# A two-layer graph network on one core: another order for the attention quads of a turn, and norms taken graph by graph at the two ends

## The chip, the core and the metric

The kernel runs on one core of a Trainium2 chip. A core has separate engines with their own instruction streams: TensorE (matrix products, "PE" in the profile, with its weight loads as "PEld"), VectorE ("DVE"), ScalarE ("ACT"), GpSimd ("POOL"), and SyncE ("SP"), which here only issues transfers (DMAs). Engines wait for each other through semaphores. Products land in PSUM, where the kernel uses eight tiles of 128 x 512 floats; everything else lives in SBUF, with 128 partitions. All arithmetic is 32-bit.

The metric is the device time of one execution, in microseconds (us), as the median of several runs.

## The reference

Sixty-four graphs of 256 nodes with 256 features each, and an integer adjacency matrix per graph, go through two layers.

```python
# layer 0: two graph attentions, then a feed-forward block
def gat(h, adj, W, a):
    Wh = h @ W
    e = leaky_relu(Wh @ a[:F] + swapaxes(Wh @ a[F:], 1, 2), 0.2)
    att = softmax(where(adj > 0, e, -9e15), axis=1)
    return att @ Wh
h = layernorm(x + gat(gat(x, adj, W1, a1), adj, W2, a2))    # first norm
x = layernorm(h + relu(h @ w_ff1 + b_ff1) @ w_ff2 + b_ff2)  # second norm

# layer 1: attention with relations, 8 heads of 32
q, k = x @ Wq + bq, x @ Wk + bk
attn = softmax(q k^T / sqrt(32))
out = sum over r of (attn * (adj == r)) @ (x @ Wv[r] + bv[r])   # adj is 0 or 1: two relations count
x = layernorm(x + out @ Wo + bo)                            # third norm
x = layernorm(x + gelu(x @ W1 + b1) @ W2 + b2)              # fourth norm
```

The hidden width of both feed-forward blocks is 1024.

## The kernel before

The graphs are taken in 32 pairs, so that a tile of features holds 512 nodes. The program is a pipeline written by hand: a fill brings the first pairs up to their stages, then 32 turns follow. In one turn (`turn(y_, x_, z)`) three pairs are at work: pair Y does attention and feed-forward of layer 1, pair X, one later, the feed-forward block of layer 0, pair Z, two later, both graph attentions of layer 0. Turn 30 has no Z, turn 31 has neither X nor Z. In turns with X the order of the instructions on TensorE, SyncE, VectorE and ScalarE is the order of the calls in the code (`tc.manual_schedule`); in turn 31 and in the fill only TensorE's and SyncE's are, and a planner places the rest. GpSimd's is the planner's throughout.

The attention of layer 1 is worked off in four *quads*: quad n is one of the two graphs (n // 2) and four of the eight heads. Each quad has these steps:

- `scores(n)`: 16 products over 32 rows into four PSUM banks (`sp`, L1015), and four exponentials on ScalarE (`e`, L1021)
- `masks(n)`: two products with the adjacency on VectorE (`ea`, L1026)
- `totals(n)`: one addition over the two halves of the nodes on VectorE (`es`, L1031)
- `sums(n)`: 32 products of the exponentials with the values into `po` (L1041) and 8 products of the totals with ones into `zo` (L1044)
- `shares(b)`, once per graph: the division (`divided`, L1052 to L1058): two transposes, a reciprocal and a product on VectorE, and one small addition on GpSimd

`values` makes the value blocks `v`, one per 128 nodes (products L999, addition of the bias on VectorE L1001). `e` and `ea` have two buffers each.

The hidden layer of a feed-forward block (`hidden_seven`) uses seven half-size products in place of eight (Strassen's scheme), each in two halves a and b. Its steps are named by product and half: `2a` makes half a of product 2, and so on; `2`, `5` and `3` of a half share a PSUM bank (`h1b`), `1`, `6`, `7` and `4` another (`h1a`). After `2`, `5` and `3` ScalarE copies the bank out (`copied`, L880), after `1`, `6` and `7` VectorE adds (`added`, L883); a product that goes on in the bank waits for that. `r`, `s` and the end of `4` are the activations on ScalarE (L914, L889). Four subtractions on VectorE (`tt`, L854) stand ahead of `hidden_seven`. In the first layer the input `hT` is the transposed, normalised pair: VectorE transposes 32 x 32 blocks (`yt`, L668), four blocks are placed by GpSimd copies (L685), twelve by DMAs on SyncE's queue (L687).

`HiddenOut` is the output product of the block, seven products again (`yf`, L960, additions to `y` L968), with sums of quarters of the hidden layer as operands (`sums`, L946).

A norm is made of statistics on VectorE (`moments`, L801 and L802), the inverse deviation on GpSimd (`rs`, L812 and L813), the shift on VectorE (`nm`, L821) and one application per 128 nodes on ScalarE (`applied_norm`, L828). Multiplication with the scale (`times`, L837) and addition of the offset (`plus`, L840) stand apart. `to_features` transposes a normalised pair on TensorE (L653), block by block, and copies it out (L654).

Six PSUM banks are handed out in turn (`bank`) to all products but `po` and `zo`, which have one each.

In the changed part of a turn pair X's scaled `y` gets its offset by a DMA that accumulates (L1209), issued by GpSimd. `early(z)` transposes pair Z's features on VectorE (`xT`, L1069), and `project` multiplies them (`xpp`, L715), half a pair at a time. `piece` takes one part of the output product that an earlier turn left over; there are such parts only in turn 31.

Of the kernel before, what the change touches and what calls it, by code (L numbers as in the profile page):

```python
# [12 lines left out]
ALU = mybir.AluOpType  # L13
# [3 lines left out]
P = 128  # L17
# [368 lines left out]
def narrow_path(  # L386
# [21 lines left out]
    G = 2  # L408
# [638 lines left out]
    def divided(u, b, po, zo, oT):  # L1047


        rz = work.tile([P, KB * N], F32, tag="s" if u < NG - 1 else "yt", name=f"rz{u}_{b}", bufs=1)  # L1050
        rq = work.tile([P, KB * N // 32], F32, tag="rq", name=f"rq{u}_{b}")
        nc.vector.transpose(rz, zo)  # L1052
        nc.vector.reciprocal(rq, rz.rearrange("p (n r) -> p n r", r=32)[:, :, 0])  # L1053
        nc.gpsimd.tensor_add(low, low, rq)  # L1054
        yield
        nc.vector.transpose(rz.rearrange("p (n r) -> p n r", r=32),
                            rq[:, :, None].to_broadcast([P, KB * N // 32, 32]))
        mark[f"divided{b}"] = nc.vector.tensor_tensor(  # L1058
            oT[:, :, b * N:(b + 1) * N], po.rearrange("p (m n) -> p m n", m=KB),
            rz.rearrange("p (m n) -> p m n", m=KB), ALU.mult)  # L1060
# [39 lines left out]

    def second_sums(z):
        d = g[z]
        for b in range(G):
            add_blocks(z, "ygp", d["y"], b,
                       lambda t, k: d["m"].s[:, t // NB * NB + k, t % NB * P:(t % NB + 1) * P],
                       lambda b, k: d["hp"][:, b * NB + k, :F], NB)
            if b == 0:
                mv = moments(z, 0, d["y"], range(NB))
        return mv
# [45 lines left out]
    def turn(y_, x_, z):  # L1155
# [24 lines left out]
        def shares(b):  # L1180
            return divided(y_, b, *acc[b], oT)

# [15 lines left out]
        with order:  # L1198
# [7 lines left out]
            if X:  # L1206
                X["hT"] = normed_features(x_, 0, X["y"])
                times(X["y"], rg1)
                nc.gpsimd.dma_start(X["y"], rb1[:, None, :].to_broadcast([P, T, F]), accum_op=ALU.add)  # L1209
            scores(0)  # L1210
            if z + 1 < NG:
                load_x(z + 1)
            if waiting:
                applied_norm(waiting[0][1], *last)
            if X:
# [3 lines left out]
            if not X:  # L1219
                masks(0)  # L1220
                totals(0)
            if X:
                v = values(y_, hT, range(T // 2, T - 1), v)
            steps = first_hidden(x_) if X else None
            scores(1)
            if not X:
                v = values(y_, hT, range(T // 2, T), v)
            masks(1)
            if not X:
                totals(1)  # L1230
            sums(0)
            if X:
                scores(2)
                first("2a 1a")
                totals(1)
                first("2b")
                masks(2, (0,))
                first("5a")
                v = values(y_, hT, range(T - 1, T), v)
                first("3a 6a")  # L1240
                masks(2, (2,))
                sums(1)
                scores(3)
                first("5b")
                totals(2)
                if Z:
                    early(z)
                first("7a 1b")
                divide = shares(0)
                next(divide)  # L1250
                first("ra 3b 6b")
                next(divide, None)
                first("4a 7b")
                if Z:
                    project(z, range(0, T // 2))
                first("rb")
                first("sa sb")
            else:
                piece()
                scores(2)  # L1260
                sums(1)
                piece()
                with behind("out"):
                    for _ in shares(0):
                        pass
                masks(2)
                totals(2)
                scores(3)
                piece()
                piece()  # L1270
            masks(3)
            totals(3)
            first("4b")
            sums(2)
            sums(3)
            if X:
                out = HiddenOut(x_, 0, X["y"], X["h1"], wf2s, out_sums(x_, 0))
                out.sums(1)
                if Z:
                    out.sums(2)  # L1280
            for _ in shares(1):
                pass
            out_(0)
            mv = moments(y_, 2, y, range(NB))
            piece()
            if Z:
                project(z, range(T // 2, T))
            if Z:
                early_adjacency(z)
            elif X:  # L1290
                out(1, 2)
                out.sums(2)
            out_(1)
            piece()
            if Z:
                first_scores(z)
            n = norm(y_, 2, y, mv=mv)
            if Z:
# [111 lines left out]
    with tc.manual_schedule(engines={mybir.EngineType.PE, mybir.EngineType.SP}):  # L1410
# [11 lines left out]
        second_softmax(1)  # L1422
        applied_norm(g[0]["y"], *norm(0, 0, g[0]["y"], mv=second_sums(0)))
        next(fold)
# [10 lines left out]
        first.sums(1, 2, 4, 3)  # L1435
        first(1, 2, 5, 6, 3, 7, 4)
        normed(0, 1, g[0]["y"])
        g[1]["n"] = norm(1, 0, g[1]["y"], mv=second_sums(1))
# [59 lines left out]
```

## Time and profile before

| | |
|---|---|
| median of 7 runs | 3083.49 us (3081.68 to 3086.09) |
| profiled execution | 3084.93 us, span 3083.3 us |
| granted TensorE clock, mean | 0.993 |
| TensorE | 3037.4 us busy, 99% of the span |
| VectorE | 2561.0 us, 83% |
| ScalarE | 1602.2 us, 52% |
| GpSimd | 685.8 us, 22% |
| a turn, from query projection to query projection | 93.55 us in most turns |

The span runs from the first to the last instruction of the profiled execution. A busy engine isn't an engine at its peak: products are pipelined, and a product that streams a little late leaves no idle time in the profile, only a larger distance to the next start. In the timeline a line is a group of equal instructions: start, time from the first's start to the last's end, engine, line, operation, output and inputs, shape, number, and in brackets the idle time of the engine before it and what ended it. In the view of waits the columns are who waited for whom, total, number and longest.

The page's row of the clock that was granted to TensorE shows full speed nearly throughout, and transfers take a small share:

```
PEclk8999999999999999999999999999999999999999
DMA  5112121221122221212211212211222212122000
```

### The profile page before, as it was taken

The numbers are of one execution on the slowest core, as the hardware profiler recorded it, in microseconds if no ns is written. First come the engines' busy times: TensorE is split into PE (matmuls) and PEld (weight loads), VectorE is DVE, ScalarE is ACT, GpSimd is POOL, SyncE is SP. The second block draws the span as 40 slices with busy tenths as digits, with TensorE's granted clock in tenths as the row PEclk, the third lists the DMA queues.
The fourth block names the chain that finished last, engine by engine and source line by source line (L and its number), as shares of the span: only waits on it lengthen the run. The fifth ranks groups of instructions, "written<-read, shape, count | busy, mean of one in ns | idle before, by whom it ended". The sixth has DMA issues, their size and how long they took to land.

```text
span 3083.3 us, 56471 instructions
## 1 busy us (share of the span) xinstructions
PE 3037.4 (99%) x21432; PEld 2341.4 (76%) x21432; DVE 2561.0 (83%) x4855; ACT 1602.2 (52%) x3212; POOL 685.8 (22%) x919
## 2 busy tenths in 40 slices
PE   7999999999999999999999999999999999999998
PEld 6678877778777778777787777787777787777866
DVE  4688888888888888888888888888888888888876
ACT  4455545554545555555555455545455555555543
POOL 3122121222211221212222212222112212122200
PEclk8999999999999999999999999999999999999999
DMA  5112121221122221212211212211222212122000
GB/s 149 20 37 43 39 45 32 51 44 38 41 42 39 45 48 33 45 33 50 44 40 42 46 32 51 44 38 41 42 39 44 48 33 45 32 51 44 19 19 16
DMA packets 444358, 129.64 MB, mean 42 GB/s; under 512 B 365065, under 2 KB 443441, under 8 KB 444081
## 3 DMA queue, kind: packets, MB, share of 16 engines
q1 hardware_dynamic: 417664, 102.46, 15.8%
q0 software_dynamic: 17424, 17.30, 3.5%
q10 hardware_dynamic: 8992, 6.19, 0.8%
q8 instruction: 172, 2.82, 0.4%
q14 instruction: 106, 0.86, 0.1%
HBM read 57.04 MB, written 16.78 MB: 24 GB/s over the span
## 4 chain that ended last, share of the span: by engine, by line
PE 88%; DVE 8%; ACT 1%; DMA 1%; issue 1%; SPq 1%; POOL 0%; DVEq 0%; ACTq 0%; POOLq 0%
PE yf L960 22%; PE h1a L871 15%; PE h1b L871 11%; PE po L1041 7%; PE vp L999 7%; PE sp L1015 4%; PE yop L786 4%; PE xpp L715 4%; PE qp L986 3%; PE kp L986 3%; PE ygp L786 3%; PE hpp L775 2%; PE zo L1044 2%; DVE s L750 2%; DVE eaq L946 1%; DVE yt L668 1%
## 5 line engine op out<-in xcount | busy, mean ns | idle before, releaser
L1021 ACT ACTIVATE e<-sp 128x512 f32<-128x512 f32 x512 | 264.4, 602 | 263.1 <-PE sp L1015 210.9
L883 DVE TENSOR_TENSOR h<-h1a,h 128x512 f32<-128x512 f32 x384 | 264.6, 690 | 159.2 <-PE h1a L871 155.8
L880 ACT COPY h<-h1b 128x512 f32<-128x512 f32 x384 | 226.4, 590 | 247.2 <-PE h1b L871 240.3
L1026 DVE TENSOR_TENSOR ea<-e,aT 128x1024 f32<-128x1024 f32 x256 | 311.2, 1246 | 32.7 <-ACT e L1021 32.7
L828 ACT ACTIVATE y<-y,nm,rs 128x256 f32<-128x256 f32 x450 | 238.7, 597 | 119.3 <-DVE nm L821 115.0
L1054 POOL TENSOR_TENSOR low<-low,rq 128x16 f32<-128x16 f32 x64 | 13.7, 214 | 1063.0 <-DVE rq L1053 1063.0
L685 POOL COPY hT<-yt 32x256 f32<-32x256 f32 x244 | 208.1, 853 | 60.1 <-DVE yt L668 50.2
L999 PE MATMUL vp<-wv,hT 128*128 128x512 f32 x480 | 218.9, 599 | 0.0
L801 DVE BATCH_NORM_STATS2 st<-y 128x6 f32<-128x256 f32 x512 | 207.9, 408 | 5.6
L968 DVE TENSOR_TENSOR y<-yf,y 128x256 f32<-128x256 f32 x448 | 183.3, 409 | 34.6 <-PE yf L960 31.0
L812 POOL TENSOR_SCALAR rs<-mv 128x4 f32<-128x4 f32 (+1 forms) x130 | 31.4, 242 | 723.5 <-DVE mv L802 636.2
L914 ACT ACTIVATE h<-h,cols 128x512 f32<-128x512 f32 x256 | 168.5, 723 | 1.5 <-DVE h L883 1.1
L988 ACT ACTIVATE q<-qp,cols 128x512 f32<-128x512 f32 x64 | 44.0, 688 | 239.7 <-PE qp L986 239.7
L837 DVE TENSOR_TENSOR y<-y,rg 128x1024 f32<-128x1024 f32 (+1 forms) x130 | 162.0, 1246 | 2.2 <-ACT y L828 1.1
L999 PEld LDWEIGHTS vp<-wv,hT 128*128 128x128 f32 x480 | 88.7, 190 | 97.6 <-issue 88.9
L1015 PEld LDWEIGHTS sp<-q,k 32*128 32x128 f32 x2048 | 98.8, 184 | 77.7 <-issue 49.8
L1031 DVE TENSOR_TENSOR es<-e 128x1024 f32<-128x1024 f32 x128 | 155.7, 1216 | 0.0
L1015 PE MATMUL sp<-q,k 32*128 32x256 f32 x2048 | 153.5, 400 | 0.0
L677 POOL COPY hT<-yt 32x256 f32<-32x256 f32 x120 | 115.9, 966 | 168.1 <-DVE yt L668 164.3
L717 ACT COPY xp<-xpp 128x260 f32<-128x260 f32 x128 | 48.1, 376 | 196.5 <-PE xpp L715 196.5
L854 DVE TENSOR_TENSOR tt<-hT 128x256 f32<-128x256 f32 x122 | 51.5, 422 | 107.6 <-DMA hT<-yt 103.5
L1041 PE MATMUL po<-e,v 128*32 128x256 f32 x2048 | 136.3, 384 | 0.0
(250 smaller groups left out, 7403.5 us busy)
## 6 DMA issues: line engine op xcount, KB each, us to landing
hT<-yt SPq DMA_DIRECT2D x912, 32.0 KB, 2.0
y<-in_x_dram SPq DMA_DIRECT2D x32, 512.0 KB, 4.6
y<-rb POOLq DMA_DIRECT2D x31, 512.0 KB, 5.3
xq<-in_x_dram SPq DMA_DIRECT2D x240, 64.0 KB, 2.2
aq<-in_adj_dram SPq DMA_DIRECT2D x240, 64.0 KB, 2.4
out_dram<-y SPq DMA_DIRECT2D x30, 512.0 KB, 2.9
hT<-yt ACTq DMA_DIRECT2D x180, 32.0 KB, 1.9
wf<-in_L_gnn_w_ff_dram SPq DMA_DIRECT2D x2, 1024.0 KB, 7.2
```

The source lines that it names most:

```text
L685: nc.gpsimd.tensor_copy(to, at)
L786: nc.tensor.matmul(ps[:, i * F:(i + 1) * F], lhs(t, k), rhs(b, k), start=(k == 0), stop=(k == n - 1))
L828: mark["normed"] = nc.scalar.activation(y[:, t, :], y[:, t, :], AF.Identity, bias=nm[:, t:t + 1], scale=rs[:, t:t + 1])
L871: nc.tensor.matmul(ps[:, i * N:(i + 1) * N], w_[:, f * P:(f + 1) * P], m, start=first and i == 0, stop=True, skip_group_check=True)
L880: mark["copied"] = nc.scalar.copy(out(h, o, b), pair(ps))
L883: mark["added"] = nc.vector.tensor_tensor(out(h, o, b), pair(one[h]), out(h, o, b), ALU.add)
L960: nc.tensor.matmul(s.ps[n][:, i * F2:(i + 1) * F2], a[:, k, i * P:(i + 1) * P], w_[:, k, :], start=n in (1, 2, 5) and i == 0 and k == 0, s ...
L999: nc.tensor.matmul(ps, hT[k][:, t * P:(t + 1) * P], wvf[:, k, :], start=(k == 0), stop=(k == KB - 1))
L1015: nc.tensor.matmul(ps[a][:, j * N:(j + 1) * N], k_[hp, m, j0:j0 + P], q[hp, m, b * N:(b + 1) * N], start=True, stop=True)
L1021: mark[f"exp{b * KB + m}"] = nc.scalar.activation(e[:, a, :], ps[a], AF.Exp, scale=isd)
L1026: nc.vector.tensor_tensor(ea[:, a:a + 2, :], e[:, a:a + 2, :], ab[:, None, :].to_broadcast([P, 2, NB * N]), ALU.mult)
L1041: nc.tensor.matmul(po[hp, m * N:(m + 1) * N], vs[:, hp], w[:, a, j * N:(j + 1) * N], start=(n == 0), stop=(n == len(terms) - 1))
```

## The change

In turns with X the first part of the turn has another order. Before, `scores(2)` stood directly behind `sums(0)`, `scores(3)` behind `sums(1)`. After, `scores(2)` comes behind the steps 2a, 1a and 5a, and `scores(3)` behind 4a, 7b and rb. The fourth values block comes directly behind the third, the second quad's totals directly behind its masks, the transpose of Z's features ahead of those masks, the first graph's division in one piece behind `sums(1)`, and Z's first projection behind `totals(3)`. The offset of X's `y` is added by VectorE ahead of `scores(3)`, in place of the accumulating DMA. The waiting pair's norm is applied after the first quad's totals.

Turns with and without X now share one sequence of calls. In turns 30 and 31 the third norm is taken graph by graph: statistics, deviation and application of the first graph, then of the second. In the fill the first norm of pair 0 is taken graph by graph too, each graph directly behind its last sums, and the second norm's first graph before the last two output products.

```diff
@@ -1052,7 +1052,6 @@
         nc.vector.transpose(rz, zo)
         nc.vector.reciprocal(rq, rz.rearrange("p (n r) -> p n r", r=32)[:, :, 0])
         nc.gpsimd.tensor_add(low, low, rq)
-        yield
         nc.vector.transpose(rz.rearrange("p (n r) -> p n r", r=32),
                             rq[:, :, None].to_broadcast([P, KB * N // 32, 32]))
         mark[f"divided{b}"] = nc.vector.tensor_tensor(
@@ -1098,13 +1097,14 @@
         d = g[z]
         d["hp"] = gat_first(z, d["m"].s, d["xp"], None if blocks[0] == 0 else d["hp"], blocks)
 
-    def second_sums(z):
+    def second_sums(z, graphs=range(G)):
         d = g[z]
-        for b in range(G):
+        mv = None
+        for b in graphs:
             add_blocks(z, "ygp", d["y"], b,
                        lambda t, k: d["m"].s[:, t // NB * NB + k, t % NB * P:(t % NB + 1) * P],
                        lambda b, k: d["hp"][:, b * NB + k, :F], NB)
-            if b == 0:
+            if b == 0 and len(graphs) == G:
                 mv = moments(z, 0, d["y"], range(NB))
         return mv
 
@@ -1178,7 +1178,7 @@
             applied(b, m, v, *e.pop(n), *acc[b])
 
         def shares(b):
-            return divided(y_, b, *acc[b], oT)
+            divided(y_, b, *acc[b], oT)
 
         def out_(b):
             add_blocks(y_, "yop", y, b, lambda t, k: oT[:, k, t * P:(t + 1) * P],
@@ -1206,12 +1206,9 @@
             if X:
                 X["hT"] = normed_features(x_, 0, X["y"])
                 times(X["y"], rg1)
-                nc.gpsimd.dma_start(X["y"], rb1[:, None, :].to_broadcast([P, T, F]), accum_op=ALU.add)
             scores(0)
             if z + 1 < NG:
                 load_x(z + 1)
-            if waiting:
-                applied_norm(waiting[0][1], *last)
             if X:
                 masks(0)
                 totals(0)
@@ -1219,82 +1216,76 @@
             if not X:
                 masks(0)
                 totals(0)
+            if waiting:
+                applied_norm(waiting[0][1], *last)
             if X:
-                v = values(y_, hT, range(T // 2, T - 1), v)
+                v = values(y_, hT, range(T // 2, T), v)
             steps = first_hidden(x_) if X else None
             scores(1)
             if not X:
                 v = values(y_, hT, range(T // 2, T), v)
+            if Z:
+                early(z)
             masks(1)
+            totals(1)
+            sums(0)
+            first("2a 1a 5a", 1)
+            scores(2)
+            sums(1)
+            if X:
+                shares(0)
+            first("3a 6a", 1)
             if not X:
-                totals(1)
-            sums(0)
+                with behind("out"):
+                    shares(0)
+            masks(2, (0,))
+            first("2b 1b")
+            masks(2, (2,))
+            first("5b 7a 3b ra 6b")
+            totals(2)
+            first("4a 7b rb")
             if X:
-                scores(2)
-                first("2a 1a")
-                totals(1)
-                first("2b")
-                masks(2, (0,))
-                first("5a")
-                v = values(y_, hT, range(T - 1, T), v)
-                first("3a 6a")
-                masks(2, (2,))
-                sums(1)
-                scores(3)
-                first("5b")
-                totals(2)
-                if Z:
-                    early(z)
-                first("7a 1b")
-                divide = shares(0)
-                next(divide)
-                first("ra 3b 6b")
-                next(divide, None)
-                first("4a 7b")
-                if Z:
-                    project(z, range(0, T // 2))
-                first("rb")
-                first("sa sb")
-            else:
-                piece()
-                scores(2)
-                sums(1)
-                piece()
-                with behind("out"):
-                    for _ in shares(0):
-                        pass
-                masks(2)
-                totals(2)
-                scores(3)
-                piece()
-                piece()
+                plus(X["y"], rb1)
+            scores(3)
+            first("sa sb", 2)
             masks(3)
             totals(3)
+            if Z:
+                project(z, range(0, T // 2))
             first("4b")
             sums(2)
             sums(3)
+            if not Z:
+                shares(1)
             if X:
                 out = HiddenOut(x_, 0, X["y"], X["h1"], wf2s, out_sums(x_, 0))
-                out.sums(1)
                 if Z:
-                    out.sums(2)
-            for _ in shares(1):
-                pass
+                    out.sums(1, 2)
+            if Z:
+                shares(1)
             out_(0)
-            mv = moments(y_, 2, y, range(NB))
+            if Z:
+                mv = moments(y_, 2, y, range(NB))
+            else:
+                n = norm(y_, 2, y, range(NB))
             piece()
             if Z:
                 project(z, range(T // 2, T))
             if Z:
                 early_adjacency(z)
             elif X:
+                out.sums(1)
                 out(1, 2)
                 out.sums(2)
             out_(1)
             piece()
             if Z:
                 first_scores(z)
-            n = norm(y_, 2, y, mv=mv)
+            if Z:
+                n = norm(y_, 2, y, mv=mv)
+            else:
+                applied_norm(y, *n)
+                n = norm(y_, 2, y, range(NB, T))
             if Z:
                 out(1)
                 Z["m"].scores(0)
@@ -1420,7 +1411,9 @@
         first_sums(1)
         next(fold)
         second_softmax(1)
-        applied_norm(g[0]["y"], *norm(0, 0, g[0]["y"], mv=second_sums(0)))
+        for b in range(G):
+            second_sums(0, (b,))
+            normed(0, 0, g[0]["y"], range(b * NB, (b + 1) * NB))
         next(fold)
         g[0]["hT"] = to_features(g[0]["y"], "h1T0")
         with behind("summed"):
@@ -1433,8 +1426,10 @@
         first_hidden(0)("2a 1a 2b 1b 5a 5b 3a 3b 6a ra 6b rb 7a sa 7b sb 4a 4b")
         first = HiddenOut(0, 0, g[0]["y"], g[0]["h1"], wf2s, out_sums(0, 0))
         first.sums(1, 2, 4, 3)
-        first(1, 2, 5, 6, 3, 7, 4)
-        normed(0, 1, g[0]["y"])
+        first(1, 2, 5, 6, 3)
+        normed(0, 1, g[0]["y"], range(NB))
+        first(7, 4)
+        normed(0, 1, g[0]["y"], range(NB, T))
         g[1]["n"] = norm(1, 0, g[1]["y"], mv=second_sums(1))
         g[0]["hT"] = to_features(g[0]["y"], "h2T0")
         affine(g[0]["y"], rg2, rb2)
```

## The prediction

> **What bounds the kernel now.** I read the page first, then the view of TensorE's own waits, the chain of waits in order of time, and last the timeline of one whole turn on each engine.
>
> ```profile
> PE 3037.4 (99%) x21432; PEld 2341.4 (76%) x21432; DVE 2561.0 (83%) x4855; ACT 1602.2 (52%) x3212; POOL 685.8 (22%) x919
> PE 88%; DVE 8%; ACT 1%; DMA 1%; issue 1%; SPq 1%; POOL 0%; DVEq 0%; ACTq 0%; POOLq 0%
> ```
>
> TensorE bounds it: 99% busy, 88% of the chain. The change adds and removes no matmul, so it can only move short stretches in which TensorE gets nothing or streams late. TensorE's own waits, in total, times and longest:
>
> ```profile
> PE yf L960 <- DVE y L968: 4.1, 4, 1.5
> PE h1T0p L653 <- ACT y L828: 3.5, 1, 3.5
> PE h1b L871 <- ACT e L1021: 3.4, 4, 0.9
> PE h2T0p L653 <- ACT y L828: 0.9, 4, 0.4
> PE h3T31p L653 <- ACT y L828: 0.8, 4, 0.3
> ```
>
> These are the waits the change touches; together some 13 us, or 0.4% of the run. Most of the loop's loss is smaller than an idle record, and shows as the distance between two starts. TensorE in turn 16:
>
> ```profile
> 1625.51 0.61 PE L1044 MATMUL zo<-es,ones 128*32 128x256 f32 x8
> 1626.05 1.15 PE L1015 MATMUL sp<-q,k 32*128 32x256 f32 x16
> 1627.15 1.11 PE L871 MATMUL h1b<-hT,wf 128*128 128x256 f32 x4
> 1628.10 1.03 PE L871 MATMUL h1a<-hT,wf 128*128 128x256 f32 x4
> 1628.96 1.03 PE L871 MATMUL h1b<-hT,wf 128*128 128x256 f32 x4
> 1629.86 1.13 PE L871 MATMUL h1b<-tt,wf1s 128*128 128x256 f32 x4
> 1630.83 1.88 PE L999 MATMUL vp<-wv,hT 128*128 128x512 f32 x4
> ...
> 1642.34 2.15 PE L871 MATMUL h1a<-tt,wf 128*128 128x256 f32 x8
> 1644.33 1.92 PE L715 MATMUL xpp<-gwe,xT 128*128 128x260 f32 x8
> ```
>
> Subtract neighbouring starts. An undisturbed step of four records takes 0.86 (1628.10 to 1628.96). Whatever is longer was late or changed the array's form. The same turn on the other engines:
>
> ```profile
> 1616.01 8.59 SPq L687 DMA_DIRECT2D hT<-yt  x12
> 1618.65 1.35 POOL L1209 DMA_DIRECT2D y<-rb  x1
> 1627.03 0.42 DVE L854 TENSOR_TENSOR tt<-hT 128x256 f32<-128x256 f32 x1 [3.19 <-DMA hT<-yt]
> 1604.09 1.22 DVE L840 TENSOR_TENSOR y<-y,rb 128x1024 f32<-128x1024 f32 x1
> ```
>
> The placing DMAs are issued until 1624.60, an accumulating 512 KB transfer goes out in the middle of them, and VectorE stands still for 3.19 until they land. Times "into the turn" below count from the first matmul of the query projection, here 1609.08.
>
> **The change, part by part.**
>
> *Bubbles that go.* (1) In the same view the second quad's scores, at 1622.46, take 1.30 to the next start, the third quad's 1.10: the fourth bank waits for VectorE's add of a values block; 0.2. (2) 5a starts 0.90 after 2b, the values block 0.97 after 5a, against 0.86: the copy of 2a stands on ScalarE behind the third quad's exponentials; 0.14. (3) The same at 3b behind the fourth quad's: the starts 1639.57, 1640.47, 1641.43 give 1.86 for two steps of 1.73; 0.14. (4) 6b to 4a 0.91; 0.05. (5) 4a and 7b take 1.99 for 1.73; 0.26. Sum 0.8 per turn.
>
> *Bubbles that come.* In the new order 5a, 5b and 3b each follow their bank's previous user after one step only. The second layer has that arrangement with an idle ScalarE: two steps h1b<-hT,w1s at 1678.62, next start 1680.42, 1.80 for 1.73. That is 0.08 for each, 0.24. 7b still stands one step behind an add: 0.22. Sum 0.46, so 0.33 is won.
>
> *Form changes.* Scores use 32 rows, sums 32 columns, all else the whole array. The half-length totals take 0.43 before more sums (1648.79 to 1649.22) and 0.54 before scores (1625.51 to 1626.05), also 0.55 before the output projection. The first step after scores takes 0.95 instead of 0.86, and scores 1.10 for passes worth 0.86. Before, second and third scores lay between sums and steps; after, scores lie between steps and sums, and sums between scores and steps. By these differences the three groups cost 1.2 now and 1.4 then: one whole form change more, 0.20 per turn. Net with the bubbles: -0.13 per turn, 31 turns: **-4.0**. Bounds: +0.2 if no bubble goes, -0.33 if the extra change is free: +6 to -10 in all. I take the middle, since each term has its own row.
>
> The Trainium skill, "TensorEngine Tiling (Array Packing)", section "Key Properties", speaks against the change: a change of tiling mode drains the array. It gives no price. At one equal price, 0.38 of a record less its 0.22 of pass, the added change would cost 0.16 per turn and the sum would be 1 us better than mine; the rows show unequal prices.
>
> *The accumulate becomes a VectorE add.* One 128x1024 add of 1.22, 31 times, 38 us of VectorE. It stands before the fourth quad's masks. Cover: VectorE idles there already (1.11 at 1639.77), and the fourth quad's totals, which end about 39.7 into the turn with the add, are needed at the last zo, now at 1650.94, 41.9 in; some 2 us of slack. Cost 0; with the cover gone up to 1.22 per turn, 38. Behind it on VectorE: masks, totals, then the hidden sums of the output product, needed later still. GpSimd's queue loses one DMA that nothing waits for early.
>
> *Late placing DMAs.* The first tt subtraction starts 16.84 to 19.1 into the turn. Step 2a starts at 18.05, so only later landings cost. The chain of waits shows it:
>
> ```profile
> 364.85 3.53 PE h1b L871 x16
> 459.24 3.53 PE h1b L871 x16
> ```
>
> 94.39 between the same steps of two turns, where most have 93.55. Turns 1 to 29 exceed 93.55 by 4.5 in all; turn 30's 2a waits another 0.8. After: 2a comes later (18.5), but the moved x transpose puts a new chain behind the landing on VectorE: four tt 1.48, transpose 1.24, two masks 2.26, totals 1.20 make 6.2; the second quad's zo needs the totals at 24.3. The landing must again come by 18.05. The accumulate no longer shares the transfer engines, so some lateness goes; the other placing phase, with no accumulate, has landings 1.4 to 1.7 late at times too. I take **-2**; bounds 0 and -5.
>
> *Moved without price.* The x transpose sooner frees the x tile sooner, so eight load DMAs (64 KB, queue time 4.2) leave about 10 us earlier, after the placing DMAs, with nothing on SyncE's queue behind them until the next placing. The fourth values block goes ahead of the second quad's scores; its add (0.68) falls into VectorE's idle 3.19. The waiting pair's four applications (2.08 of ScalarE) go behind the first totals; ScalarE has 2.42 idle there. The first graph's division runs whole, ahead of 6a's add: VectorE is waiting for that step.
>
> *Fill.* First norm per graph: transposes are spaced 0.49 by four applications; two remain behind the last statistics, -0.98, less an added small nm and rs in the chain: -0.7. Second norm: the transposes' wait, 0.39 plus three spacings of 0.49 for 0.11, falls by -1.3, but statistics now stand before the last yf products, whose wait of 0.8 becomes 1.7: +0.9. Together **-1.1**; bounds +1 and -3. TensorE's granted clock was 0.50 from 65 to 70 us, right after the idle 3.5 for h1T0p, and 0.58 from 70 to 75.
>
> The Trainium skill, "TensorE: Matmul & The Clock Gate", section "Why this matters for your kernels", asks for no idle gap over about 3 us; the new gap would be 2.8. If that kept full clock, four steps that took 5.14 there would take 3.5, and the sum would be 1.6 better; I don't count on it.
>
> *Turn 30.* With no projection between, 4b stands directly behind 7b's add:
>
> ```profile
> 2956.89 1.13 PE L871 MATMUL h1a<-tt,wf 128*128 128x256 f32 x4 [0.81 <-DVE h L883]
> ```
>
> The step starts 1.1 late; the fourth quad's scores now lie between: -1.1 + 0.2 of form = **-0.9**. *Turn 31.* The h3T31 transposes start 0.49 apart three times behind four applications; two remain: -1.0 + 0.1 for an added nm: **-0.9**.
>
> **Sum.** -4.0 - 2 - 1.1 - 0.9 - 0.9 = -8.9 on the profiled execution's 3084.93 (span 3083.3): 3076.0. That execution is 1.44 above the median of the seven runs, 3083.49, so the forecast for a median is 3074.6, rounded **3075**.
>
> **The rivals.** About 0.2% (6.2 us) is what a measurement of this kernel can tell from no change: faster means below 3077.3, slower above 3089.7.
>
> A, slower: the new VectorE chain behind the landing makes zo of the second quad wait. For: in turn 16 tt starts 17.95 into the turn, 0.1 from the limit. Against: without the accumulate landings should be sooner. It decides from a landing of 18.5 in every turn (15 us over 31 turns); at 18.9 it costs 0.85 each, 26: about 3101.
>
> B, no difference: the form changes eat the bubbles, or the copies wait elsewhere. Loop 0 and no landing gained: 3075 + 4 + 2 = 3081; for it: 0.33 and 0.20 are near each other.
>
> C, more: all lateness goes (-5) and the fill keeps full clock (-1.6), with turn 0, 96.4 long, falling to 93.5 (-2.9): 3075 - 3 - 1.6 - 2.9 = 3067.5.
>
> D, slower: the added add delays the fourth masks by more than its 2 us of slack, because adds ahead of it come late. At 0.6 a turn 18: 3093; all of it 38: 3113.
>
> **How the numbers follow.** My forecast has 0.52, its own range 3069 to 3080; B 0.20, C 0.10, A 0.12, D 0.06. Five sixths of the first lie below 3077.3, with C 0.54 faster; its rest and B give 0.28; A and D 0.18. From 3064 to 3092 the range leaves out a third of C and most of A and D, under 0.2.
>
> **What would show it.** Right: a normal turn of 93.4; no 0.81 at 4b in turn 30; second quad's scores 1.1; h3T31p waits under 0.3; fewer turns over 94. Wrong: an idle record at zo or po after VectorE's totals or masks (A, D); turns at 93.55 or above with steps of 0.95 (B). The forecast fails most easily on the loop: 0.3 per turn mis-sized is 9 us.

## The result, and the profile after

The changed kernel takes 3075.31 us (median of 14 runs, 3073.8 to 3076.98), the kernel before 3084.33 us (34 runs, 3079.63 to 3086.67). The ratio is 0.9971, 95% interval 0.9964 to 0.9978: faster by 9.0 us or 0.29%. The forecast was 3075. The total is right; of the five terms that made it up, two were well off, and their errors nearly cancelled. The experiments below were timed in three groups, each with the kernel before beside it (3084.15, 3081.87 and 3084.12), so that ratios compare better across groups than times do.

Profiled spans are 3083.3 before and 3075.3 after. First the page's lines on busy time and on the chain of the changed kernel:

```profile
PE 3032.9 (99%) x21432; PEld 2331.7 (76%) x21432; DVE 2597.8 (84%) x4890; ACT 1601.4 (52%) x3212; POOL 648.1 (21%) x896
PE 91%; DVE 7%; DMA 1%; POOL 1%; issue 1%; ACT 1%; SPq 0%; ACTq 0%; POOLq 0%; DVEq 0%
```

TensorE is still the bound, with 91% of the chain in place of 88%. VectorE got 36.8 us more work, the 31 added adds, and GpSimd 38 us less. TensorE's own waits in the changed kernel (total, times, longest):

```profile
PE yf L960 <- DVE y L968: 4.9, 4, 1.5
PE h1T0p L653 <- ACT y L828: 3.5, 3, 2.2
PE sp L1015 <- ACT k L988: 2.0, 1, 2.0
PE h3T31p L653 <- ACT y L828: 0.2, 1, 0.2
PE h2T0p L653 <- ACT y L828: 0.2, 1, 0.2
```

The waits of 2a (L871) are gone. Before, they were 3.4 on the exponentials and 1.6 on the placing DMAs, the latter by this line of the kernel before:

```profile
PE h1b L871 <- DMA hT<-yt: 1.6, 2, 1.0
```

The waits of the third norm in turn 31 and of h2T0p are nearly gone. The wait of h1T0p is as long in total as it was, in three pieces now, the yf products of the fill wait longer, and a new one of 2.0 has come: scores wait for the bias of the keys. It occurs once, in turn 0.

Turn 16 of the changed kernel on TensorE, from the second quad's scores on:

```profile
1621.83 1.15 PE L1015 MATMUL sp<-q,k 32*128 32x256 f32 x16
1622.91 1.07 PE L1041 MATMUL po<-e,v 128*32 128x256 f32 x16
...
1625.20 1.13 PE L871 MATMUL h1b<-hT,wf 128*128 128x256 f32 x4
1626.17 1.03 PE L871 MATMUL h1a<-hT,wf 128*128 128x256 f32 x4
1627.04 1.10 PE L871 MATMUL h1b<-tt,wf1s 128*128 128x256 f32 x4
1628.07 1.15 PE L1015 MATMUL sp<-q,k 32*128 32x256 f32 x16
...
1638.61 2.15 PE L871 MATMUL h1a<-tt,wf 128*128 128x256 f32 x8
1640.69 1.15 PE L1015 MATMUL sp<-q,k 32*128 32x256 f32 x16
```

Subtract the starts: the second quad's scores take 1.08 (1.30 before). 5a takes 1.03 to the scores behind it; with the 0.08 of lateness that the prediction gave it, 0.09 is left for the change of form. 4a and 7b take 2.08 to the next scores: 1.73, the 0.26 of lateness that they had before, and again 0.09. The same turn on VectorE:

```profile
1622.55 0.41 DVE L854 TENSOR_TENSOR tt<-hT 128x256 f32<-128x256 f32 x1
...
1641.41 1.22 DVE L840 TENSOR_TENSOR y<-y,rb 128x1024 f32<-128x1024 f32 x1
1643.03 2.36 DVE L1026 TENSOR_TENSOR ea<-e,aT 128x1024 f32<-128x1024 f32 x2 [0.41 <-ACT e L1021]
1645.31 1.22 DVE L1031 TENSOR_TENSOR es<-e 128x1024 f32<-128x1024 f32 x1
```

The subtraction no longer waits for the landing: it starts 15.82 into the turn, behind VectorE's own work. The added add stands in front of an idle 0.41. The totals end at 1646.53; the last zo of the turn starts at 1648.49, so some 2 us are left.

Where the 8.0 of span went, from the starts of the query projections in the two profiles:

| stretch | before | after | difference |
|---|---|---|---|
| fill and turn 0 | 202.47 | 204.57 | +2.1 |
| turns 1 to 29, usual turn | 93.55 | 93.44 | -0.11 each, -3.2 |
| turns 1 to 29, what some lasted longer | 4.6 | 1.0 | -3.6 |
| turn 30 | 75.97 | 73.83 | -2.1 |
| turn 31 to the end | 87.37 | 86.14 | -1.2 |

### The profile page after: what moved, and what is told of

The parts are those of the page before. It is cut to its first block, busy times and chain, and to the rows that moved or that the text cites. A ratio compares the mean times of both kernels' runs of the same rounds, so it can differ in the third digit from the quotient of the medians.

```text
span 3075.3 us, 56424 instructions
## 1 busy us (share of the span) xinstructions
PE 3032.9 (99%) x21432; PEld 2331.7 (76%) x21432; DVE 2597.8 (84%) x4890; ACT 1601.4 (52%) x3212; POOL 648.1 (21%) x896
## 4 chain that ended last, share of the span: by engine, by line
PE 91%; DVE 7%; DMA 1%; POOL 1%; issue 1%; ACT 1%; SPq 0%; ACTq 0%; POOLq 0%; DVEq 0%
PE yf L960 22%; PE h1a L871 15%; PE h1b L871 11%; PE po L1041 8%; PE vp L999 7%; PE sp L1015 4%; PE xpp L715 4%; PE qp L986 4%; PE yop L786 4%; PE kp L986 3%; PE ygp L786 3%; PE hpp L775 2%; PE zo L1044 2%; DVE s L750 1%; DVE yt L668 1%; DVE eaq L946 1%
## 5 line engine op out<-in xcount | busy, mean ns | idle before, releaser
L840 DVE TENSOR_TENSOR y<-y,rb 128x1024 f32<-128x1024 f32 (+1 forms) x130 | 166.8, 1283 | 3.2
L1015 PEld LDWEIGHTS sp<-q,k 32*128 32x128 f32 x2048 | 92.5, 184 | 74.2 <-issue 44.8
L1015 PE MATMUL sp<-q,k 32*128 32x256 f32 x2048 | 146.6, 400 | 2.0 <-ACT k L988 2.0
L813 POOL TENSOR_TENSOR rs<-rs,mhalf 128x4 f32<-128x4 f32 (+1 forms) x134 | 134.3, 1002 | 8.3
```

The lines of the kernel that those rows point to most:

```text
L1015: nc.tensor.matmul(ps[a][:, j * N:(j + 1) * N], k_[hp, m, j0:j0 + P], q[hp, m, b * N:(b + 1) * N], start=True, stop=True)
```

## The experiments

Theory: the loop's gain has two independent parts, the order (0.1 per turn) and the accumulating transfer that kept the placing DMAs late; the ends gain by the norm graph by graph; the fill does not. Rivals: the order alone ended the long turns; the added add isn't free; and, for the fill, that its loss is an accident of one execution.

**The add alone, in the old order.**

```diff
 before:
-                nc.gpsimd.dma_start(X["y"], rb1[:, None, :].to_broadcast([P, T, F]), accum_op=ALU.add)
 ...
                 first("sa sb")
+                plus(X["y"], rb1)
```

> The kernel before with one part of the change: the offset of X's y is added by VectorE (behind sa sb, ahead of the fourth quad's masks) and no DMA accumulates; the order of the quads is the old one. Theory 1 (the accumulating transfer makes the placing DMAs late): first tt at 15.8 to 17.5 us into the turn in nearly every turn, none past 18.05, turns of 93.55 without the long ones; total 4 to 6 us less than before (ratio about 0.9984), the add itself free. Theory 2 (landings scatter for another reason): long turns as before, ratio 1.000. Theory 3 (the added 1.22 us of VectorE reaches the last zo): turns up to 94.8, ratio up to 1.012.

Measured: 3079.57, the kernel before beside it 3084.15, ratio 0.9987 (0.9978 to 0.9996). The usual turn lasts 93.53, no first tt starts after 18.0 in turns 1 to 29, and these turns last 2712.9 in place of 2717.5. So 4.6 of the gain comes from taking the transfer away (0.7 of it is the usual turn), and the add costs nothing in that place either. Theory 1 holds, with little to spare: the latest first tt starts at 17.94.

**The accumulating DMA back, in the new order.**

```diff
 after:
                 times(X["y"], rg1)
+                nc.gpsimd.dma_start(X["y"], rb1[:, None, :].to_broadcast([P, T, F]), accum_op=ALU.add)
 ...
-            if X:
-                plus(X["y"], rb1)
             scores(3)
```

> The changed kernel with the accumulating DMA put back in place of VectorE's add; the new order stays. Theory 1: undisturbed turns stay at 93.44, but landings past 18 come back and some turns last 0.3 to 1 us longer: 3 to 5 us more than the changed kernel, ratio to before about 0.9985. Theory 2 (the new order, not the transfer, ended the long turns): as the changed kernel, ratio 0.997.

Measured: 3078.96, ratio 0.9982 (0.9973 to 0.9991), 3.6 over the changed kernel. Undisturbed turns stay at 93.44, and the earliest first tt starts 16.82 into the turn, behind its landing, where it is 15.82 without the transfer, behind VectorE's own work: the transfer makes the landing at least 1.0 later. The time is lost where SyncE issues the placing DMAs. Its twelve issues in turn 16, in the changed kernel and then in this one:

```profile
1613.66 7.54 SPq L687 DMA_DIRECT2D hT<-yt  x12
```

```profile
1614.30 8.58 SPq L687 DMA_DIRECT2D hT<-yt  x12
```

Both start 6.93 into the turn. An issue takes 0.59, but with the transfer two of them, behind GpSimd's, take 1.07 and 1.15. A block issued just ahead of those lands after 4.35 in place of 1.89, but what counts is the last one: over turns 1 to 29 the last issue starts at 14.90 or later with the transfer and at 13.86 or later without. Why an issue takes longer then, no run shows.

Five turns of 1 to 29 are long by landing: the first tt starts 18.25, 18.48, 18.70, 18.75 and 19.06 into them, and they last 0.24, 0.48, 1.06, 1.02 and 1.06 longer than 93.44. Three pay just what they exceed 18.0 by; why the two at 18.7 pay 0.3 more stays open. Turn 6 of this kernel, on TensorE and then on VectorE:

```profile
689.94 1.10 PE L871 MATMUL h1b<-hT,wf 128*128 128x256 f32 x4 [0.55 <-DMA hT<-yt]
...
696.04 0.64 PE L1044 MATMUL zo<-es,ones 128*32 128x256 f32 x8
```

```profile
689.90 0.42 DVE L854 TENSOR_TENSOR tt<-hT 128x256 f32<-128x256 f32 x1 [3.16 <-DMA hT<-yt]
...
694.77 1.22 DVE L1031 TENSOR_TENSOR es<-e 128x1024 f32<-128x1024 f32 x1
```

2a waits 0.55 for the landing itself, and the second quad's totals end at 695.99, just ahead of their zo at 696.04: that is the rest. The price starts at about 18.0, where the prediction had put it for both orders, and it is rival A's mechanism. The scatter itself isn't the transfer's: in turns 6, 13, 20 and 27 the subtraction starts 3.5 to 4.1 behind the last issue, and in the add's kernel above, which has no such transfer, the same four turns show it too. There the issues are 1.0 sooner, and none passes 18.0. In the changed kernel no turn exceeds 2.7; what makes those four landings late stays open.

**The third norm of turns 30 and 31 whole.**

```diff
 after:
-            if Z:
-                mv = moments(y_, 2, y, range(NB))
-            else:
-                n = norm(y_, 2, y, range(NB))
+            mv = moments(y_, 2, y, range(NB))
 ...
-            if Z:
-                n = norm(y_, 2, y, mv=mv)
-            else:
-                applied_norm(y, *n)
-                n = norm(y_, 2, y, range(NB, T))
+            n = norm(y_, 2, y, mv=mv)
```

> The changed kernel with the third norm of turns 30 and 31 taken over both graphs at once, as before. If the norm graph by graph is what shortened the end: turn 31 1.0 longer, turn 30 0.2 longer, 1.2 in all, ratio to before about 0.9975. If the end became shorter by the other order of the quads alone: no difference, ratio 0.997.

Measured: 3077.34, ratio 0.9978 (0.9969 to 0.9987), 2.0 over the changed kernel. In its profile turn 30 lasts 74.14 (0.3 longer) and turn 31 88.83 (2.7 longer). About 1.0 of this is the four transposes behind four applications. The rest is the clock. The first hidden steps behind them, then the windows 3038 to 3040, 3040 to 3042 and 3042 to 3044 (the column ahead of the last two is the granted clock):

```profile
3037.78 1.62 PE L871 MATMUL h1b<-h3T,w 128*128 128x256 f32 x4 [0.78 <-DVE h3T L654]
3039.20 1.91 PE L871 MATMUL h1a<-h3T,w 128*128 128x256 f32 x4
```

```profile
3038.00:3040.00 2.00, 2.00 (x6) 1.62 (x6) 2.00 (x4) 1.48 (x3) 0.00 (x0) 0.57 0.00 0
3040.00:3042.00 2.00, 2.00 (x7) 1.59 (x6) 2.00 (x4) 0.03 (x1) 0.00 (x0) 0.58 0.00 0
3042.00:3044.00 2.00, 2.00 (x11) 1.77 (x10) 1.90 (x4) 0.59 (x1) 0.00 (x0) 1.00 0.37 131
```

A step that lasts 0.86 took 1.70 there. The add in the old order, which has the norm whole too, shows the same (turn 31 88.77); the profile of the kernel before does not (87.37). So the norm graph by graph removed 1.0, as expected, and with it a halved clock that costs another 1.7 in two of the three profiles with the norm whole and in none of those with it graph by graph.

**The third quad's scores directly behind the first quad's sums again.**

```diff
 after:
             sums(0)
-            first("2a 1a 5a", 1)
             scores(2)
+            first("2a 1a 5a", 1)
             sums(1)
```

> The changed kernel with the third quad's scores back directly behind the first quad's sums; all else new. If the copy of 2a behind the exponentials was the price of that place: 5a late by 0.04 to 0.14 per turn again, one change of the array's form less (0.1 to 0.2), turns of 93.35 to 93.5. Rival: one of the new neighbours depends on it (the exponentials come early, banks are short): a wait of some 0.3 or more per turn, turns of 93.8, ratio to before about 1.000.

Measured: 3105.01, ratio 1.007 (1.0056 to 1.0084); the usual turn 94.37, 0.93 more. The price is larger than even the rival said, but the cause is the one the first expectation named, the copy of 2a. TensorE's waits of this kernel:

```profile
PE h1b L871 <- ACT h L880: 23.2, 31, 0.7
```

5a needs the copy of 2a, which now stands on ScalarE behind four exponentials (2.06), with only 1a to cover it. The kernel before had the same queue, but 2b stood there as well, and 5a and the product behind it lost 0.14. By these two orders the place of the scores is not good or bad by itself: what counts is how many steps cover the copy.

**More of the add.** The offset line stands twice, and then four times, in each turn with X.

```diff
 after:
                 plus(X["y"], rb1)
+                plus(X["y"], rb1)
```

> The changed kernel with the offset of X's y added twice in each of the 31 turns (its values are zeros): one more VectorE add of 1.14 ahead of the fourth quad's masks, 35 us of VectorE in all. By the slack read from the trace (the fourth totals end 1.96 ahead of the last zo, VectorE idles 0.41 ahead of the masks) nothing: ratio 0.997. If VectorE's length counts: 1.14 per turn, 35 us, ratio 1.0085.

> The same with three more adds: 3.42, less 0.41 of idle time, 3.0 later. That exceeds the slack of 1.96 by 1.0 at the last zo, and the division behind it makes the second output projection late by some 0.7 more: 1.0 to 2.0 per turn, 31 to 62 us over the changed kernel, ratio to before 1.007 to 1.017. If there is no such chain: ratio 0.997; if VectorE's length counts: 3.4 per turn, ratio 1.031.

Measured: one more, 3074.92, ratio 0.998 (0.997 to 0.9989), usual turn 93.44, to a hundredth that of the changed kernel (turn 30 alone is 0.6 longer). Three more, 3143.74, ratio 1.0204 (1.0189 to 1.022), usual turn 95.63: 2.19 each, a little above the range. The waits of the latter:

```profile
PE po L1041 <- DVE ea L1026: 16.9, 32, 1.5
PE yop L786 <- ACT xp L717: 12.2, 22, 0.6
...
PE yop L786 <- DVE q L1057: 4.5, 8, 0.6
```

The slack covers a second add. With four the price comes in two places: in turn 16 the fourth quad's sums, which wait for the masks, take 1.4 longer than with one more add, where 1.0 was expected, and the second output projection, which needs the second graph's division, starts 0.7 later still. So rival D's chain exists, but one add doesn't reach it.

**The fill's norms whole.**

```diff
 after:
-        for b in range(G):
-            second_sums(0, (b,))
-            normed(0, 0, g[0]["y"], range(b * NB, (b + 1) * NB))
+        applied_norm(g[0]["y"], *norm(0, 0, g[0]["y"], mv=second_sums(0)))
 ...
-        first(1, 2, 5, 6, 3)
-        normed(0, 1, g[0]["y"], range(NB))
-        first(7, 4)
-        normed(0, 1, g[0]["y"], range(NB, T))
+        first(1, 2, 5, 6, 3, 7, 4)
+        normed(0, 1, g[0]["y"])
```

> The changed kernel with both norms of the fill taken over the two graphs at once, as before. The prediction's price for the graph-by-graph fill was a gain of 1.1 (by it: 1.1 slower than the changed kernel, ratio to before 0.9975). The traces say a loss: fill and turn 0 together last 202.5 in the kernel before and 200.9 with the first run's old fill, but 204.6, 203.6, 203.3 and 204.8 with the new one; by them 1.5 to 3 us less than the changed kernel, ratio 0.9963.

Measured: 3072.62, ratio 0.9973 (0.9963 to 0.9983), with the kernel before at 3081.87. The kernel that follows, which turned out to be the changed kernel again, took 3073.96 beside it: 1.3 more, with ranges that overlap. The times alone would not decide. The profiles do: fill and turn 0 together last 198.96 here, and 200.89 and 202.47 in the two kernels of the old order, but 202.82 to 204.83 in all seven profiles with the new fill and GpSimd's work where it was (that with four adds left out, since they lengthen turn 0 themselves). So the new fill loses: 1.3 by this pair of medians, 3.0 by the means of the profiles.

**GpSimd's weights later.** In the fill GpSimd scales and folds layer 1's hidden weights, ahead of the inverse deviation of turn 0's norm.

```diff
 after:
         shifted(w1, range(FB // 2, FB), lb3, b1, "b1")
+        yield
         scaled(w1, lg3)
 ...
                 times(X["y"], rg1)
+            if y_ == 0:
+                next(fold)
```

> The changed kernel, but GpSimd's scaling and folding of layer 1's hidden weights is issued in turn 0 behind pair 1's transposes, not ahead of that pair's norm; the work is the same. Theory: GpSimd's queue (two scalings of 4.2 and a fold ahead of the inverse deviation) sets the shift at 114.1, hence the wait of 2.0 of turn 0's first scores and the landing at 20.2 into the turn; without it the wait goes and turn 0 falls from 97.3 to about 94.5 to 95.5: 2 to 3 us less than the changed kernel. Rival: h2T's copy or the half clock holds the turn anyway: less than 0.5.

Measured: 3073.96, ratio 0.9976 (0.9967 to 0.9985). The edit did nothing: the planner, which orders GpSimd's queue, put the same instructions in the same places. It counts as a second execution of the changed kernel. It shows the mechanism more clearly than the first, on GpSimd and on TensorE (the added lines shift this kernel's line numbers by one):

```profile
103.26 4.22 POOL L599 TENSOR_SCALAR w<-w,cols 128x1024 f32<-128x1024 f32 x2 [3.76 <-PE b1sp L592]
107.56 0.25 POOL L813 TENSOR_SCALAR rs<-mv 128x4 f32<-128x4 f32 x1
107.78 1.26 POOL L569 TENSOR_TENSOR w1s<-w 128x512 f32<-128x512 f32 x1
108.99 1.03 POOL L814 TENSOR_TENSOR rs<-rs,mhalf 128x4 f32<-128x4 f32 x1
```

```profile
103.24 3.68 PE L987 MATMUL qp<-h2T,wq 128*128 128x512 f32 x8
106.75 3.60 PE L987 MATMUL kp<-h2T,wk 128*128 128x512 f32 x8
114.01 2.09 PE L1016 MATMUL sp<-q,k 32*128 32x256 f32 x16 [3.66 <-ACT k L989]
116.03 9.19 PE L1000 MATMUL vp<-wv,h2T 128*128 128x512 f32 x16
```

Two scalings (4.22) and a fold (1.26) stand ahead of the deviation; ScalarE applies the norm ahead of the keys' bias, and the first scores wait for that bias. From b1sp's start to those scores it is 12.5 in all eight profiles with the new fill and this queue, whether TensorE comes early or late. With the old fill it is 12.1 to 12.4, but there TensorE itself is late: its query projection, behind the spaced transposes, takes 5.9 to 6.5 at a lowered clock, and it hardly waits at the scores (0.2 at most). With the new fill the projection takes 3.68 in five profiles, and TensorE waits 3.66 at the other end; in the three others it takes 5.38, and the wait is that much shorter, 1.97. The changed kernel's own profile is one of these:

```profile
107.25 5.38 PE L986 MATMUL qp<-h2T,wq 128*128 128x512 f32 x8
118.03 1.15 PE L1015 MATMUL sp<-q,k 32*128 32x256 f32 x16 [1.97 <-ACT k L988]
```

After a wait of 3.66 the clock is halved: scores 2.09 for 1.15, values 9.19 for 7.13.

**The same, tied by an order that holds.** The folding is tied behind GpSimd's own block copies of turn 0.

```diff
 after:
         shifted(w1, range(FB // 2, FB), lb3, b1, "b1")
+        w2s.extend(seven_out(w2, "w2"))
+        yield
         scaled(w1, lg3)
         w1s.extend(seven(w1, "w1"))
-        w2s.extend(seven_out(w2, "w2"))
 ...
-                    nc.gpsimd.tensor_copy(to, at)
+                    mark["diagonal"] = nc.gpsimd.tensor_copy(to, at)
 ...
                 times(X["y"], rg1)
+            if y_ == 0:
+                with behind("diagonal"):
+                    next(fold)
```

Beside it ran the same with both fill norms whole, the same with only the first norm whole, and the changed kernel.

> The changed kernel with GpSimd's scaling and folding of layer 1's hidden weights tied behind the block copies of turn 0 (the run before this one asked for that order and did not get it). Theory: turn 0's inverse deviation then starts at about the end of the statistics, 3.7 to 4.2 earlier plus a fold of 1.26, the first scores' wait of 2.0 to 3.7 goes, the half clock behind the longer of these waits with it, and the landing comes before 18.05: fill and turn 0 together from 203.3 to 204.8 down to 198 to 200; 4 to 5 us less than the changed kernel on the same chip. Rival: the wait moves on (queries' bias, half clock on the projections): less than 1.

> The same with both norms of the fill taken whole. If the graph-by-graph fill lost only because GpSimd's queue held turn 0's first scores, it should now win by what it gained at h2T0, about 1 us: this run 1 slower than the one with the new fill. If its loss of 1.5 to 3 is in the fill itself: this run that much faster.

> The same with only the first norm of the fill whole, the second graph by graph. By the trace the first norm graph by graph is worth 0.4 behind its sums: within 1 us of the run with the new fill. If the first norm is what costs: 1 to 2 faster.

> The changed kernel once more, as the base of the three runs beside it and as one more look at its fill: ratio to before 0.997, fill and turn 0 together 203 to 205 (203.5 in the run whose GpSimd order was the same).

Measured, with the kernel before at 3084.12 (fill and turn 0 from the profiles):

| kernel | median, range | ratio to before | fill and turn 0 |
|---|---|---|---|
| changed, again | 3075.46 (3073.83 to 3077.15) | 0.9971 (0.9960 to 0.9982) | 204.02 |
| fold behind | 3071.10 (3069.06 to 3074.35) | 0.9958 (0.9944 to 0.9971) | 201.65 |
| fold behind, first norm whole | 3071.74 (3070.85 to 3072.99) | 0.9960 (0.9946 to 0.9973) | 198.08 |
| fold behind, both norms whole | 3076.50 (3074.22 to 3078.86) | 0.9977 (0.9968 to 0.9986) | 202.76 |

With the fold out of the way the changed kernel gains 4.4, as expected, and the wait at the first scores is gone. Fill and turn 0 in its profile are 1.7 above the expected range, but that execution is the slowest of the five, 3.25 over their median, with a query projection of 5.38. The move has a price, too: from the first scores on, turn 0 takes 87.8 in the profiles of all three kernels with the fold behind, and 86.5 in those of the kernel before and of the changed kernel. VectorE's four subtractions (`tt`) now run beside the fold, and in this kernel three of them take 1.04 to 1.49 for 0.42. GpSimd and TensorE of the fold-behind kernel (line numbers again one higher):

```profile
105.42 1.05 POOL L813 TENSOR_SCALAR rs<-mv 128x4 f32<-128x4 f32 x1 [4.08 <-DVE mv L803]
106.56 1.95 POOL L814 TENSOR_TENSOR rs<-rs,mhalf 128x4 f32<-128x4 f32 x1
113.78 2.66 POOL L686 COPY hT<-yt 32x256 f32<-32x256 f32 x4 [5.28 <-DVE yt L669]
116.55 5.06 POOL L599 TENSOR_SCALAR w<-w,cols 128x1024 f32<-128x1024 f32 x2
```

```profile
110.30 3.60 PE L987 MATMUL kp<-h2T,wk 128*128 128x512 f32 x8
113.83 1.15 PE L1016 MATMUL sp<-q,k 32*128 32x256 f32 x16
```

The fill's second norm graph by graph now wins: with it whole as well the kernel is about 5 us slower than with only the first whole. That is more than the 1 expected; in the profile of the former the query projection behind the spaced transposes takes 6.64, in that of the latter 3.68. The first norm makes no difference that these runs show (0.6 between the medians; the 3.6 between the two profiles is mostly the slow execution above). So the graph-by-graph fill is worth something only once GpSimd's queue does not hold turn 0. The version with the fold behind beats both kernels.

## Why the prediction was right, and where it was not

*What bounds the kernel*, and that the change could only move short stretches on TensorE: right.

*Bubbles and form changes, -4.0.* Nearly right: the usual turn is 0.11 shorter, 0.13 was forecast; 0.09 of it is left when the add alone, in the old order, is the base. The single terms show in the starts above: 1.30 to 1.08 at the second quad's scores, 0.08 at 5a, 0.26 still at 7b. The bounds of +6 to -10 were not needed. The third-quad run adds that the gain belongs to this order as a whole: moving one part back cost 0.93 per turn.

*The extra form change.* The Trainium skill, "TensorEngine Tiling (Array Packing)", "Key Properties", says that a change of tiling mode drains the array, without a price. The one equal price that the prediction tried came to 0.16 per turn, its rows to 0.20. In the new order a step takes 0.09 more when scores follow it. No run here prices a change of mode by itself, so 0.16 and 0.20 can't be told apart.

*The added add at no cost.* Right, and the slack of 2 us as well: one more add was still free, three more were not. Rival D fell.

*Late placing DMAs, -2.* The transfer did make the landings late, and the limit of 18.0 was right too; the size was not. The prediction had the two share the transfer engines; what the traces show is SyncE's issues, 1.0 later in all. The step that was mis-sized is the estimate that "some lateness goes", with a second half left for other causes. It all went: -3.6 in turns 1 to 29 and 0.8 in turn 30, -4.4 in all, near the bound of -5. Taking away the transfer alone gave -4.6 in the old order, and putting it back cost 3.6 in the new one. The second placing phase, which was the reason for keeping half, is still up to 1.1 late in the changed kernel (its first subtraction starts 63.2 to 64.4 into the turn), so it is late for other reasons and was no evidence on the first. That all of it went has some luck in it: the four late landings of the add's kernel stopped 0.1 to 0.6 short of 18.0. Rival A fell because the landings came earlier once the transfer was gone.

*Fill, -1.1.* Wrong in sign. Two of its four terms were right: the yf products wait 0.9 longer (1.43 in place of 0.52, by the lines below, before and after), and h2T0p's transposes and their wait fell. From that wait's start to the query projection it is 10.7 before and 9.9 after.

```profile
95.83 2.05 PE L960 MATMUL yf<-wf2t,h 128*128 128x128 f32 x16 [0.52 <-DVE y L968]
```

```profile
98.82 2.05 PE L960 MATMUL yf<-wf2t,h 128*128 128x128 f32 x16 [1.43 <-DVE y L968]
```

What failed was the step from there to the end of the fill: that what TensorE gains at h2T0p is gained for the run. GpSimd's queue, which the prediction followed only up to the fill's norms, sets turn 0's first scores 12.5 us behind b1sp, and the scalings in it became slower (4.2 for 3.2). Turn 0, counted like any other turn, got 0.9 longer, and 3.7 to 3.9 longer in four other profiles, those with the wait of 3.66 and the usual turn of 93.44. The size of 2.1 in the table is partly an accident of that profile: the first ygp product, ahead of anything that was changed in the fill, starts at 52.70 before and at 54.11 after, but at 51.56 to 53.56 in eight other executions with the new fill. What the loss is without it, the runs bound only to 1 to 3.

*The clock in the fill.* The prediction did not count on the better clock, and that was right. The Trainium skill, "TensorE: Matmul & The Clock Gate", "Why this matters for your kernels", asks for no idle gap over about 3 us. At h1T0p the gap of 3.52 became three, of 1.13, 0.16 and 2.24, with transposes between, and still the clock granted was 0.66 from 65 to 70 us and 0.50 from 70 to 75. The same page, "Part 4: PE-mode transpose", says that transposes do not count as busy in the same way; the halved steps behind the spaced transposes of turn 31 agree with that, 1.70 for 0.86, but only in two profiles of three: the kernel before has the same spacing and kept its clock there. The wait of 3.66 in turn 0 halved the clock, that of 1.97 did not.

*Turn 30, -0.9.* -1.3 besides the landing: 4b no longer idles, and yf waits 1.06 in place of 1.30. *Turn 31, -0.9.* -1.2; with the clock's risk more.

So the sum was right by chance. On the profiles' difference, -8.0 for a forecast of -8.9, the landings brought 2.4 more than forecast and the ends 0.7; fill and turn 0 took 3.2 and the order fell 0.8 short. Rival C had the first half right, that all lateness would go; the fill's clock and a shorter turn 0, its other half, did not come.

## What to carry to other kernels

A transfer that is issued amid small, urgent ones should be priced by what the small ones lose, not by its own landing: here 31 accumulations that looked hidden cost 3.6 to 4.6 us, and an add on a busy engine, at a place with slack, cost none. A gain at the end of a stage counts only after every queue that the next stage waits for has been followed from the same point, that of the slow engine with set-up work above all. And an order that a planner decides is to be read after the edit, not assumed.

## What had not been expected of the hardware

VectorE and GpSimd run slower beside each other. In the fill VectorE's masked products (L750, 128 x 256) take 0.41 alone and 0.93 to 1.49 while GpSimd adds or folds weights, though still 0.41 beside some of its scalings. GpSimd's two scalings of 128 x 1024 took 3.2 beside VectorE's addition (the three profiles with the old fill), 4.2 beside its multiplication and addition, and 5.06 beside its masks and totals. With the new fill the multiplication falls under the scalings, which is part of why the chain behind b1sp is slower.

A halved clock outlasts the idle time that brought it and can cost nearly as much again: in turn 0 a wait of 3.66 was followed by 3.0 of slower products (0.94 at the scores, 2.06 at the values), where a wait of 1.97 was followed by none. In the profiles with 1.97 the clock had been low just before, at the query projection: 1.7 had been lost there instead.
